# Two low-degree nodes per counting slot in a graph layer: counts in ones and 256s, copied as 16-bit integers and read as bytes

## The chip, the cores and the metric

The kernel runs on one core of a Trainium2 chip. The metric is the device time of one execution in microseconds; the median of several runs is compared. An execution that was profiled gives the profile: every instruction with its engine, start, duration and what it waited for. The engines are TensorE (PE, with weight loads shown as PEld), VectorE (DVE), ScalarE (ACT), GpSimd (POOL) and SyncE (SP). SP only issues DMAs; POOL issues the indirect ones, which gather rows.

## The reference

`x` has 12,500 nodes of 128 features. There are 200,000 edges, each with a source, a destination and one of four types; they are sorted by destination, and the destinations are dense at small numbers (the node number goes as a uniform number squared).

```
h    = max(layernorm(x), 0)
msgs = h[src] @ W[type] + b[type]          # per edge
out  = x + segment_sum(msgs, dst)
```

## The kernel before

**Two ways for edges.** The edges lie in 1563 chunks of 128. The first 464 chunks (59,392 edges, destinations below 1144) go the *dense* way, because each of these nodes has many edges: for each node the kernel counts how many edges come from each source node with each type, and multiplies the counts with the table of all `h`. The other 1099 chunks go the *gathered* way.

**The gathered way** (`gather`, line 397, and `sum_up`, line 414). POOL gathers 128 rows per chunk with one indirect DMA (line 403) into `hm`, eight chunks to a buffer, five buffers. PE sums the rows of a chunk by type and destination (line 461, one-hots made by DVE at line 424), ACT copies the sums (line 468), PE applies `W` (line 475), and DVE adds the result to a ring of destinations (line 487). Groups have 16 chunks; there are 71 groups, the last four of 12, 8, 4 and 3 chunks. The first eight groups are "raw": they gather rows of `x` and normalize them, while the table `htab` of `h`, split into three bf16 parts, is being written to DRAM. From group 8 on the rows come from `htab`.

**The dense way** (`count`, line 725, `multiply`, line 757). A *slot* is up to 128 edges of one node, one per partition. `loT` and `hkT` hold for each slot (a column) the source's row number (0 to 127) and a number made of its block (0 to 97) and the edge's type. For each slot DVE makes two one-hot tiles, 128 wide from `loT` (line 737) and 392 wide from `hkT` (line 738), and PE multiplies them (line 742): a 128 x 392 table of counts in PSUM. A few nodes have more than one slot; two slots at most accumulate into one table, and a node with more is treated as several *virtual* nodes whose results are added. ACT then copies the table as 8-bit floats into `counts` (line 745) and sums it along the way, to check that no count is too large. There are 1336 slots and 1180 virtual nodes, so 1336 pairs of one-hots and matmuls and 1180 copies.

`multiply` reads the whole table `htab` once per batch of nodes, in 25 loads of up to 384 KB on SP (line 763, five buffers), and multiplies the three parts with `counts` (line 766, 294 matmuls of up to 368 columns), then with `W` (line 779), and adds to `acc` (line 784). The 15 batches have 23, 46, eleven times 92, 53 and 46 virtual nodes.

**The order.** `dense_work` (line 806) interleaves `count` of one batch with `multiply` of the batch before, in equal progress. The main loop (line 846) goes through the groups; after each quarter of a group it takes steps of the dense work until their share of PE columns reaches `pace` (line 793), so that the sum of a group's own columns and its dense columns is the same for each group from 8 to `FULL - 3` (64). What is left is done at group 65. The slots are built during the raw groups by `make_slots` (line 599), whose last steps run just before group 8. When the dense work is done, `leave` (line 496) transposes `acc`, adds `x` and stores the rows, and `check_all` (line 554) combines the checks into one flag; if it is set, a slow and general version runs at the end.

Of the kernel before, what the change touches and what calls it, by code (L numbers as in the profile page):

```python
# [31 lines left out]
F32 = mybir.dt.float32  # L35
BF16 = mybir.dt.bfloat16
F16 = mybir.dt.float16
F8 = mybir.dt.float8e4
I32 = mybir.dt.int32
AF = mybir.ActivationFunctionType  # L40
ALU = mybir.AluOpType
AX = mybir.AxisListType
# [4 lines left out]
P = 128  # L47
# [8 lines left out]
VBMAX = 92  # L56
# [11 lines left out]
def kernel(  # L68
# [44 lines left out]
        return next((n for n in range(12, WIN, 4) if (n - 1) * a_node > P + 6 * P**0.5), WIN)  # L113

    NDT = -(-ND // P)
    virtual = [(k, d) for k in range(0, len(levels), 2) for d in range(levels[k])]

    virtual = virtual[ND - 2 * VBMAX : ND] + virtual[: ND - 2 * VBMAX] + virtual[ND:]
    VB = VBMAX
    sizes_of = [VB // 4, VB // 2]  # L120
    left = len(virtual) - sum(sizes_of) - VB // 2
    sizes_of += [VB] * (left // VB) + ([left % VB] if left % VB else []) + [VB // 2]
    batches = [virtual[sum(sizes_of[:i]) :][:n] for i, n in enumerate(sizes_of)]
    NB = NW * NT


# [427 lines left out]
    def check_all():  # L554

        low = const.tile([P, BM], F32, name="low")
        step = const.tile([P, BM], F32, name="step")
        nc.vector.memset(low, 0.0)
        for (ja, jb, _), i in zip(flushes, goes):
            if starts[i] + sizes[i] < TM:  # L560
                nc.vector.tensor_scalar(
                    step, rowf, starts[i] + sizes[i] - 0.5, (jb - ja) * float(P), ALU.is_gt, ALU.mult
                )
                nc.vector.tensor_add(low, low, step)
        bad = const.tile([P, 5], F32, name="bad")
# [10 lines left out]
        many = const.tile([P, 2], F32, name="many")  # L576
        nc.vector.tensor_reduce(many[:, 0:1], bad, AX.X, ALU.add)
        nc.vector.tensor_copy(many[:, 1:2], seen)
        pb = x_ps.tile([P, 2], F32, name="pt")
        nc.tensor.matmul(pb, ones, many, start=True, stop=True)  # L580
        sums_ok = const.tile([P, 2], F32, name="sums_ok")
        nc.vector.tensor_single_scalar(sums_ok[:, 0:1], pb[:, 0:1], 0.5, op=ALU.is_gt)
        nc.vector.tensor_single_scalar(sums_ok[:, 1:2], pb[:, 1:2], 3.0 * E0, op=ALU.not_equal)
        nc.vector.tensor_reduce(flag, sums_ok, AX.X, ALU.max)


# [12 lines left out]
    def make_slots(dix):  # L599
# [79 lines left out]
        def unpack(a, z):  # L679
            n = z - a  # L680
            hk = dix.tile([P, 512], I32, name="hk")
            nc.vector.tensor_single_scalar(hk[:, :n], packed[:, a:z], 7, op=ALU.arith_shift_right)
            nc.vector.tensor_copy(hkT[:, a:z], hk[:, :n])
            nc.vector.scalar_tensor_tensor(
                loT[:, a:z], hkT[:, a:z], float(-P), packed[:, a:z], op0=ALU.mult, op1=ALU.add
            )

            nc.vector.tensor_single_scalar(hk[:, :n], hk[:, :n], NT - 1, op=ALU.bitwise_and)
            ohs = []
            for t in range(NT):  # L690
                is_t = dix.tile([P, 512], BF16, name="is_t", bufs=NT)
                if t < NT - 1:
                    nc.vector.tensor_single_scalar(is_t[:, :n], hk[:, :n], t + 1.0, op=ALU.is_equal)
                else:
                    nc.vector.tensor_single_scalar(is_t[:, :n], hkT[:, a:z], 0.5, op=ALU.is_gt)
                ohs.append(is_t)
            yield True
            pn = x_ps.tile([N3, 512], F32, name="pt")
            for t in range(NT):
                nc.tensor.matmul(pn[:, :n], pick_a[:, t, :], ohs[t][:, :n], start=(t == 0), stop=(t == NT - 1))  # L700
            nc.scalar.copy(cnt12[:, a:z], pn[:, :n])

        for a, z in pieces(NS):
            yield from unpack(a, z)
            yield True
        nc.vector.memset(seen, 0.0)
        nc.vector.tensor_reduce(seen[:N3], cnt12, AX.X, ALU.add)

# [15 lines left out]

    def count(vs, counts):
        todo = []
        for i, (k, d) in enumerate(vs):
            todo.append((i, starts_of[k] + d, True, not (k + 1 < len(levels) and d < levels[k + 1])))
            if not todo[-1][3]:
                todo.append((i, starts_of[k + 1] + d, False, True))  # L730
        both = sdp.tile([P, VB], F32, name="both", bufs=2)
        for s0 in range(0, len(todo), OB):
            part = todo[s0 : s0 + OB]
            o1 = ohp.tile([P, OB, P], BF16, name="o1")
            o2 = ohp.tile([P, OB, NB], BF16, name="o2")
            for k, (i, s, first, last) in enumerate(part):
                nc.vector.tensor_scalar(o1[:, k, :], iota_b, loT[:, s : s + 1], None, ALU.is_equal)  # L737
                nc.vector.tensor_scalar(o2[:, k, :], iota_n, hkT[:, s : s + 1], None, ALU.is_equal)  # L738
            for k, (i, s, first, last) in enumerate(part):
                if first:  # L740
                    pb = x_ps.tile([P, NB], F32, name="pt")
                nc.tensor.matmul(pb, o1[:, k, :], o2[:, k, :], start=first, stop=last)  # L742
                if last:

                    nc.scalar.activation(  # L745
                        counts[:, :, i * NT : (i + 1) * NT],
                        pb.rearrange("p (b t) -> p b t", t=NT),
                        AF.Copy,
                        accum_out=both[:, i : i + 1],
                        saturate=True,  # L750
                    )
                yield (s0 + k + 1) / len(todo)
        top = sdp.tile([P, 1], F32, name="top")
        nc.vector.tensor_reduce(top, both[:, : len(vs)], AX.X, ALU.max)
        nc.vector.tensor_max(most, most, top)

    def multiply(vs, counts):
        nv = len(vs)
        pa = a_ps.tile([P, VB * NT], F32, name="pa")
        for j0 in range(0, NW, HB):  # L760
            j1 = min(j0 + HB, NW)
# [10 lines left out]
                    )  # L772
            if j1 < NW:
                yield j1 / NW
        sd = sdp.tile([P, VB, NT], F32, name="sd")
        nc.scalar.copy(sd[:, :nv].rearrange("p v t -> p (v t)"), pa[:, : nv * NT])
        py = y_ps.tile([P, VB], F32, name="py")
        for t in range(NT):
            nc.tensor.matmul(py[:, :nv], wsb[:, t, :], sd[:, :nv, t], start=(t == 0), stop=(t == NT - 1))  # L779
        i = 0  # L780
        while i < nv:
            k, d = vs[i]
            n = next((m for m in range(1, nv - i) if vs[i + m] != (k, d + m)), nv - i)
            nc.vector.tensor_tensor(acc[:, d : d + n], acc[:, d : d + n], py[:, i : i + n], ALU.add)
# [7 lines left out]

    def pace(gi, part):

        last = FULL - 2
        if gi >= last:
            return 2.0
        own = [columns(i) for i in range(RAW, last)]
# [2 lines left out]
        return ((n + part) * a_group - sum(own[:n]) - part * own[n]) / dense_columns()  # L801

    def dense_columns():
        return NS * float(NB) + len(virtual) * NW * 3.0 * NT

    def dense_work():

# [5 lines left out]
        for vs in batches + [None]:  # L813
            steps = {}
            now = None
            if vs:
                now = vs, dense.tile([P, NW, VB * NT], F8, name="counts")
                slots = sum(1 + (k + 1 < len(levels) and d < levels[k + 1]) for k, d in vs)
                steps[count(*now)] = slots * a_slot
# [12 lines left out]
            before = now  # L832

    seen = const.tile([P, 1], F32, name="seen")
    slots = mid.enter_context(tc.tile_pool(name="slots", bufs=1, side="right"))
    loT = slots.tile([P, NS], F32, name="loT")
    hkT = slots.tile([P, NS], F32, name="hkT")
    building = ExitStack()
    dix = building.enter_context(tc.tile_pool(name="dix", bufs=1, side="right"))
    to_slots = make_slots(dix)  # L840
# [5 lines left out]
    for gi, (t0, g) in enumerate(zip(starts, sizes)):  # L846
# [85 lines left out]
        if gi == RAW - 1:  # L932
# [11 lines left out]
            most = sdp.tile([P, 1], F32, name="most")  # L944
            nc.vector.memset(most, 0.0)
            work = dense_work()
        for (ja, jb, _), i in zip(flushes, goes):
            if i == gi:
# [135 lines left out]
```

## Time and profile before

| | |
|---|---|
| median of 3 runs | 1467.21 us (1465.16 to 1470.11) |
| profiled execution, its own time | 1466.72 us |
| its span, first to last instruction | 1465.0 us |
| mean granted PE clock | 0.950 |
| busy: PE, DVE, ACT, POOL | 1305.8, 1055.8, 860.7, 1078.9 us |
| HBM read and written | 263.84 MB, 16.03 MB |

The page of the profile lists, for groups of instructions, the line, engine and operation, the tiles written and read, shapes, how often, then busy time, mean duration in ns, and idle time of the engine before them with what ended it. Durations of neighbouring instructions on one engine can overlap, so that starts, not durations, tell how often an engine takes one. The row of tenths gives busy shares in 40 slices of the run.

### The profile page before, as it was taken

What the parts mean: (1) busy time and instruction counts of PE and PEld (TensorE: products, weight loads), DVE (VectorE), ACT (ScalarE), POOL (GpSimd) and SP (SyncE); (2) the same over time, 40 slices, a digit from 0 to 9 for tenths busy, and PEclk for the clock granted to TensorE, in tenths of its full rate; (3) what the DMA queues carried; (4) which work ended last, traced back from release to release, by engine and by line L of the source; (5) the groups of instructions that cost most, each with busy time, mean ns of one, the idle gap of its engine ahead of it and who ended that gap; (6) DMA issues with size and microseconds to landing.
All of it is one profiled execution on the core that took longest, in us unless ns stands there. A gap on an engine that the chain in (4) does not pass through costs nothing.

```text
span 1465.0 us, 32946 instructions
## 1 busy us (share of the span) xinstructions
PE 1305.8 (89%) x10222; PEld 866.6 (59%) x10222; DVE 1055.8 (72%) x5728; ACT 860.7 (59%) x3026; POOL 1078.9 (74%) x1109
## 2 busy tenths in 40 slices
PE   1566787998999999999999999999999999999964
PEld 0444455765666556666666666666666666677743
DVE  8796878879889877677675786757787676677233
ACT  7776447867545566566655666646766665445010
POOL 7777775677677767777777777777777777777773
PEclk9995768999999999999999999999999999999977
DMA  7643247975566567676676767776676667777841
GB/s 214 181 138 115 89 149 245 299 231 173 154 193 176 165 183 204 190 225 200 202 205 196 210 186 207 199 200 201 192 209 193 190 194 212 216 237 252 304 121 54
DMA packets 141833, 282.11 MB, mean 193 GB/s; under 512 B 26995, under 2 KB 74661, under 8 KB 141653
## 3 DMA queue, kind: packets, MB, share of 16 engines
q1 hardware_dynamic: 90949, 176.07, 38.3%
q0 software_dynamic: 50704, 103.91, 26.3%
q8 instruction: 80, 1.31, 0.3%
q14 instruction: 100, 0.82, 0.2%
HBM read 263.84 MB, written 16.03 MB: 191 GB/s over the span
## 4 chain that ended last, share of the span: by engine, by line
PE 70%; DVE 11%; ACT 4%; DMA 3%; POOL 2%; issue 2%; DVEq 0%; ACTq 0%; POOLq 0%
PE pa L766 35%; PE pt L742 13%; PE py L475 9%; PE ps L461 8%; ACT counts L745 3%; DVE o L738 3%; DVE o L737 2%; POOL hm L403 2%; DVE ring L487 2%; DMA hs<-htab 2%; DVE oh L424 2%; DMA hm<-htab,srcT 1%; PE ps L444 1%; PE ps L446 1%; PE py L779 1%
## 5 line engine op out<-in xcount | busy, mean ns | idle before, releaser
L403 POOL DMA_INDIRECT hm<-htab,srcT x971 | 947.0, 975 | 322.4 <-issue 266.9
L766 PE MATMUL pa<-counts,hs 128*128 128x368 fp8e4 (+3 forms) x4410 | 713.2, 299 | 7.2 <-DMA hs<-htab 6.4
L745 ACT ACTIVATE counts<-pt 128x392 fp8e4<-128x392 f32 x1180 | 574.7, 519 | 169.7 <-PE pt L742 165.8
L766 PEld LDWEIGHTS <-hs 128*128 128x128 bf16 x4410 | 404.3, 99 | 232.4 <-issue 31.7
L738 DVE TENSOR_SCALAR o<-iota_n,hkT 128x392 bf16<-128x392 f16 x1336 | 450.3, 337 | 0.0
L737 DVE TENSOR_SCALAR o<-iota_b,loT 128x128 bf16<-128x128 bf16 x1336 | 346.8, 260 | 128.5 <-PE pt L742 126.7
L742 PE MATMUL pt<-o,o 128*128 128x392 bf16 x1336 | 368.0, 333 | 11.4 <-ACT counts L745 3.9
L745 ACT ACTIVATION_READ_ACCUMULATOR counts<-pt 128x1 f32 x1180 | 268.7, 228 | 0.0
L487 DVE TENSOR_TENSOR ring<-ring,py 128x16 f32 (+4 forms) x1072 | 187.3, 175 | 106.8 <-PE py L475 89.8
L468 ACT COPY sb<-ps 128x320 f32<-128x320 f32 (+4 forms) x275 | 115.8, 424 | 234.1 <-PE ps L461 210.0
L424 DVE TENSOR_SCALAR oh<-iota_b,keyT 128x64 bf16<-128x64 bf16 (+4 forms) x971 | 179.2, 265 | 90.1 <-PE ps L461 88.2
L461 PE MATMUL ps<-oh,hm 128*128 128x80 bf16 (+4 forms) x2913 | 160.0, 202 | 20.9 <-DMA hm<-htab,srcT 19.8
L461 PEld LDWEIGHTS <-hm 128*128 128x128 bf16 x2913 | 136.8, 99 | 59.1 <-DMA hm<-htab,srcT 26.2
L742 PEld LDWEIGHTS <-o 128*128 128x128 bf16 x1336 | 125.5, 99 | 78.0 <-DVE o L738 13.0
L475 PE MATMUL py<-sb,wsb 128*128 128x384 f32 (+4 forms) x536 | 170.9, 454 | 0.3 <-ACT sb L468 0.3
L403 POOL DMA_INDIRECT hm<-in_x_dram,srcT x128 | 130.4, 1019 | 40.8 <-issue 36.9
L475 PEld LDWEIGHTS py<-sb,wsb 128*128 128x128 f32 x536 | 107.0, 211 | 38.3 <-issue 13.7
L450 ACT CAST cnt<-ps 128x256 bf16<-128x256 f32 (+7 forms) x71 | 29.3, 413 | 130.0 <-PE ps L446 112.4
L461 PE MATMUL ps<-ohf,hm 128*128 128x48 f32 x256 | 59.0, 391 | 51.5 <-ACT hm L365 51.5
L461 PEld LDWEIGHTS ps<-ohf,hm 128*128 128x128 f32 x256 | 52.8, 298 | 69.0 <-ACT hm L365 55.7
L365 ACT ACTIVATE hm<-hm,nmr,rstd 128x128 f32<-128x128 f32 x128 | 51.0, 481 | 6.3 <-DVE nmr L356 6.3
L473 PE MATMUL py<-cnt,b 128*128 128x256 bf16 (+5 forms) x67 | 20.7, 309 | 24.0 <-DVE ring L487 22.8
(173 smaller groups left out, 551.7 us busy)
## 6 DMA issues: line engine op xcount, KB each, us to landing
hs<-htab SPq DMA_DIRECT2D x360, 384.0 KB
hm<-htab,srcT POOLq DMA_INDIRECT x971
htab<-h SPq DMA_DIRECT2D x11, 768.0 KB
xo<-in_x_dram SPq DMA_DIRECT2D x23, 256.0 KB
out_dram<-xo SPq DMA_DIRECT2D x23, 256.0 KB
xt<-in_x_dram SPq DMA_DIRECT2D x6, 512.0 KB
hs<-htab SPq DMA_DIRECT2D x15, 192.0 KB
xt<-in_x_dram SPq DMA_DIRECT2D x5, 448.0 KB
```

Of the source, the lines that this page charges most:

```text
L365: nc.scalar.activation(h(k), xt(k), AF.Relu, bias=nmr[:r, k : k + 1], scale=rstd[:r, k : k + 1])
L403: nc.gpsimd.indirect_dma_start(out=rows[:, (i - h0) * width : (i - h0 + 1) * width], out_offset=None, in_=table, in_offset=bass.IndirectOf ...
L424: nc.vector.tensor_scalar(oh[:, i, :], (iota_f if raw else iota_b)[:, :K], keyf[:, t0 + i : t0 + i + 1], None, ALU.is_equal)
L461: mm = nc.tensor.matmul(ps[:, i - i0, :], rows(i, c, nparts), oh[:, i, :], start=(c == 0), stop=(c == nparts - 1),)
L468: nc.scalar.copy(sb[:, i0:i1].rearrange("p g t n -> p g (t n)"), ps[:, : i1 - i0, :])
L475: mm = nc.tensor.matmul(py[:, :g, :], wsb[:, t, :], sb[:, :g, t, :], start=False, stop=(t == NT - 1))
L487: nc.vector.tensor_tensor(to, to, py[:, i, :], ALU.add)
L737: nc.vector.tensor_scalar(o1[:, k, :], iota_b, loT[:, s : s + 1], None, ALU.is_equal)
L738: nc.vector.tensor_scalar(o2[:, k, :], iota_n, hkT[:, s : s + 1], None, ALU.is_equal)
L742: nc.tensor.matmul(pb, o1[:, k, :], o2[:, k, :], start=first, stop=last)
L745: nc.scalar.activation(counts[:, :, i * NT : (i + 1) * NT], pb.rearrange("p (b t) -> p b t", t=NT), AF.Copy, accum_out=both[:, i : i + 1], ...
L766: nc.tensor.matmul(pa[:, : nv * NT], hs[:, j - j0, c * D : (c + 1) * D], counts[:, j, : nv * NT], start=(j == 0 and c == 0), stop=(j == NW ...
```

## The change

**Pairs.** Nodes from `PAIRS` = 558 up to 1143 have so few edges that two neighbours together fit 128 partitions. As edges are sorted, the edges of the two lie in different partitions of their two columns, so the columns of `loT` and `hkT` are added into one, and `byT` holds 1 in the partitions of the first node and 256 in those of the second. One pair of one-hots and one matmul then count both; the one-hot from `loT` is multiplied by `byT`. The other ("alone") nodes are also put in twos: each keeps its own slots, the second's one-hots are multiplied by the constant 256, and both accumulate into the same table.

**One copy for two.** The table holds (ones) + 256 x (the second's). ACT copies it once as 16-bit unsigned integers. `multiply` reads the same bytes as 8-bit floats: the low byte is the first node, the high byte the second. A byte n up to 16, read as such a float, is n / 512, so the later copy scales by 512. The sums along the way are taken apart with integer operations on DVE at the end of a batch, and a further check compares the total number of counted edges with the expected one.

**Order.** The first two batches (22 and 46 nodes) take shared pairs only; the others mix alone and shared nodes in proportion. There are 1043 slots and 590 copies. Slots per batch: before 23, 46, 92, 161, 160, eight times 92, 53, 65; after 11, 23, 121, 121, 107, then 70 or 71 eight times, 52, 44. `pace` spreads the dense work over one group more (`FULL - 1`). The one-hots of `make_slots` share a pool of buffers.

```diff
+    PAIRS = next(
+        d
+        for d in range(levels[1] + levels[1] % 2, ND, 2)
+        if (lambda m: m + 6 * m**0.5)(E * (((d + 2) / N) ** 0.5 - (d / N) ** 0.5)) <= P
+    )
+    alone = [(k, d) for k in range(0, len(levels), 2) for d in range(min(levels[k], PAIRS))]
+    shared = [(0, d) for d in range(PAIRS, ND)]
...
+    sizes_of = [VB // 8 * 2, VB // 4 * 2]
+    left = len(alone) + len(shared) - sum(sizes_of) - VB // 4 * 2
+    sizes_of += [VB] * (left // VB) + ([left % VB] if left % VB else []) + [VB // 4 * 2]
+    batches = []
+    a = b0 = 0
+    for i, n in enumerate(sizes_of):
+        na, ns = len(alone) - a, len(shared) - b0
+        n1 = 0 if i < 2 else min(round(n * na / (na + ns) / 2) * 2, na)
+        n1 = max(n1, n - ns)
+        batches.append(alone[a : a + n1] + shared[b0 : b0 + n - n1])
+        a, b0 = a + n1, b0 + n - n1
...
+    def slots_of(u):
+        if u[0] is not None and u[0][0] == 0 and u[0][1] >= PAIRS:
+            return [(u[0][1], None)]
+        got = []
+        for v, by in zip(u, (1.0, 256.0)):
+            if v is not None:
+                k, d = v
+                got.append((starts_of[k] + d, by))
+                if k + 1 < len(levels) and d < levels[k + 1]:
+                    got.append((starts_of[k + 1] + d, by))
+        return got
...
+        one, two = slice(PAIRS, ND, 2), slice(PAIRS + 1, ND, 2)
+        nc.vector.tensor_scalar(byT, hkT[:, two], 0.5, 255.0, ALU.is_gt, ALU.mult)
+        nc.vector.tensor_single_scalar(byT, byT, 1.0, op=ALU.add)
+        for of in (loT, hkT):
+            nc.vector.tensor_tensor(of[:, one], of[:, one], of[:, two], ALU.add)
...
-                nc.vector.tensor_scalar(o1[:, k, :], iota_b, loT[:, s : s + 1], None, ALU.is_equal)
+                if by == 1.0:
+                    nc.vector.tensor_scalar(o1[:, k, :], iota_b, loT[:, s : s + 1], None, ALU.is_equal)
+                else:
+                    if by is None:
+                        by = byT[:, (s - PAIRS) // 2 : (s - PAIRS) // 2 + 1]
+                    nc.vector.tensor_scalar(o1[:, k, :], iota_b, loT[:, s : s + 1], by, ALU.is_equal, ALU.mult)
                 nc.vector.tensor_scalar(o2[:, k, :], iota_n, hkT[:, s : s + 1], None, ALU.is_equal)
...
                         accum_out=both[:, i : i + 1],
-                        saturate=True,
...
-        nc.vector.tensor_reduce(top, both[:, : len(vs)], AX.X, ALU.max)
-        nc.vector.tensor_max(most, most, top)
+        n = len(vs) // 2
+        nc.vector.tensor_copy(bi[:, :n], both[:, :n])
+        nc.vector.tensor_single_scalar(bb[:, 0, :n], bi[:, :n], 255, op=ALU.bitwise_and)
+        nc.vector.tensor_single_scalar(bb[:, 1, :n], bi[:, :n], 8, op=ALU.arith_shift_right)
+        nc.vector.tensor_copy(bf[:, :, :n], bb[:, :, :n])
+        nc.vector.tensor_reduce(top[:, 0:1], bf[:, :, :n], AX.XY, ALU.max)
+        nc.vector.tensor_reduce(top[:, 1:2], bf[:, :, :n], AX.XY, ALU.add)
+        nc.vector.tensor_max(most, most, top[:, 0:1])
+        nc.vector.tensor_add(held, held, top[:, 1:2])
...
+        counts = counts.bitcast(F8)
...
-        nc.scalar.copy(sd[:, :nv].rearrange("p v t -> p (v t)"), pa[:, : nv * NT])
+        nc.scalar.activation(
+            sd[:, : nv // 2].rearrange("p v t m -> p (v t m)"), pa[:, : nv * NT], AF.Copy, scale=512.0
+        )
...
-        last = FULL - 2
+        last = FULL - 1
...
-                now = vs, dense.tile([P, NW, VB * NT], F8, name="counts")
+                now = vs, dense.tile([P, NW, VB // 2 * NT], U16, name="counts")
```

More of the change, by code (lines that the diff above doesn't have):

```diff
@@ L39 @@
 I32 = mybir.dt.int32
+U16 = mybir.dt.uint16
 AF = mybir.ActivationFunctionType
@@ L115, with units @@
     NDT = -(-ND // P)
-    virtual = [(k, d) for k in range(0, len(levels), 2) for d in range(levels[k])]
-    virtual = virtual[ND - 2 * VBMAX : ND] + virtual[: ND - 2 * VBMAX] + virtual[ND:]
-    VB = VBMAX
[L120 to L123, printed above, removed]
+    PAIRS = next(
[4 more added lines that the diff above has]
+    alone = [(k, d) for k in range(0, len(levels), 2) for d in range(min(levels[k], PAIRS))]
+    if len(alone) % 2:
+        alone.append(None)
+    shared = [(0, d) for d in range(PAIRS, ND)]
+    VB = VBMAX
+    sizes_of = [VB // 8 * 2, VB // 4 * 2]
[9 more added lines that the diff above has]
+        a, b0 = a + n1, b0 + n - n1
+    assert a == len(alone) and b0 == len(shared)
+    def slots_of(u):
[9 more added lines that the diff above has]
+        return got
+    def units(vs):
+        return [tuple(vs[i : i + 2]) for i in range(0, len(vs), 2)]
+    NSLOTS = sum(len(slots_of(u)) for vs in batches for u in units(vs))
     NB = NW * NT
@@ L575, in check_all @@
         nc.vector.tensor_single_scalar(bad[:, 4:5], most, MANY + 0.5, op=ALU.is_gt)
-        many = const.tile([P, 2], F32, name="many")
+        many = const.tile([P, 3], F32, name="many")
         nc.vector.tensor_reduce(many[:, 0:1], bad, AX.X, ALU.add)
         nc.vector.tensor_copy(many[:, 1:2], seen)
-        pb = x_ps.tile([P, 2], F32, name="pt")
+        nc.vector.tensor_copy(many[:, 2:3], held)
+        pb = x_ps.tile([P, 3], F32, name="pt")
         nc.tensor.matmul(pb, ones, many, start=True, stop=True)
-        sums_ok = const.tile([P, 2], F32, name="sums_ok")
+        sums_ok = const.tile([P, 3], F32, name="sums_ok")
         nc.vector.tensor_single_scalar(sums_ok[:, 0:1], pb[:, 0:1], 0.5, op=ALU.is_gt)
         nc.vector.tensor_single_scalar(sums_ok[:, 1:2], pb[:, 1:2], 3.0 * E0, op=ALU.not_equal)
+        nc.vector.tensor_single_scalar(sums_ok[:, 2:3], pb[:, 2:3], float(E0), op=ALU.not_equal)
         nc.vector.tensor_reduce(flag, sums_ok, AX.X, ALU.max)
@@ L690, in unpack @@
             for t in range(NT):
-                is_t = dix.tile([P, 512], BF16, name="is_t", bufs=NT)
+                is_t = dix.tile([P, 512], BF16, name="sel", bufs=2 * DENSE)
                 if t < NT - 1:
@@ L726, in count @@
         todo = []
[L727 to L731, printed above, removed]
+        for i, u in enumerate(units(vs)):
+            of = slots_of(u)
+            todo += [(i, c, by, n == 0, n == len(of) - 1) for n, (c, by) in enumerate(of)]
+        both = sdp.tile([P, VB // 2], F32, name="both", bufs=2)
         for s0 in range(0, len(todo), OB):
@@ L735, in count @@
             o2 = ohp.tile([P, OB, NB], BF16, name="o2")
-            for k, (i, s, first, last) in enumerate(part):
-                nc.vector.tensor_scalar(o1[:, k, :], iota_b, loT[:, s : s + 1], None, ALU.is_equal)
+            for k, (i, s, by, first, last) in enumerate(part):
+                if by == 1.0:
[4 more added lines that the diff above has]
+                    nc.vector.tensor_scalar(o1[:, k, :], iota_b, loT[:, s : s + 1], by, ALU.is_equal, ALU.mult)
                 nc.vector.tensor_scalar(o2[:, k, :], iota_n, hkT[:, s : s + 1], None, ALU.is_equal)
-            for k, (i, s, first, last) in enumerate(part):
+            for k, (i, s, by, first, last) in enumerate(part):
                 if first:
@@ L749, in count @@
                         accum_out=both[:, i : i + 1],
-                        saturate=True,
                     )
                 yield (s0 + k + 1) / len(todo)
-        top = sdp.tile([P, 1], F32, name="top")
-        nc.vector.tensor_reduce(top, both[:, : len(vs)], AX.X, ALU.max)
-        nc.vector.tensor_max(most, most, top)
+        n = len(vs) // 2
+        bi = sdp.tile([P, VB // 2], I32, name="bi")
+        nc.vector.tensor_copy(bi[:, :n], both[:, :n])
+        bb = sdp.tile([P, 2, VB // 2], I32, name="bb")
+        nc.vector.tensor_single_scalar(bb[:, 0, :n], bi[:, :n], 255, op=ALU.bitwise_and)
+        nc.vector.tensor_single_scalar(bb[:, 1, :n], bi[:, :n], 8, op=ALU.arith_shift_right)
+        bf = sdp.tile([P, 2, VB // 2], F32, name="bf")
+        nc.vector.tensor_copy(bf[:, :, :n], bb[:, :, :n])
+        top = sdp.tile([P, 2], F32, name="top")
+        nc.vector.tensor_reduce(top[:, 0:1], bf[:, :, :n], AX.XY, ALU.max)
+        nc.vector.tensor_reduce(top[:, 1:2], bf[:, :, :n], AX.XY, ALU.add)
+        nc.vector.tensor_max(most, most, top[:, 0:1])
+        nc.vector.tensor_add(held, held, top[:, 1:2])
     def multiply(vs, counts):
         nv = len(vs)
+        counts = counts.bitcast(F8)
         pa = a_ps.tile([P, VB * NT], F32, name="pa")
@@ L774, in multiply @@
                 yield j1 / NW
-        sd = sdp.tile([P, VB, NT], F32, name="sd")
-        nc.scalar.copy(sd[:, :nv].rearrange("p v t -> p (v t)"), pa[:, : nv * NT])
+        sd = sdp.tile([P, VB // 2, NT, 2], F32, name="sd")
+        nc.scalar.activation(
+            sd[:, : nv // 2].rearrange("p v t m -> p (v t m)"), pa[:, : nv * NT], AF.Copy, scale=512.0
+        )
         py = y_ps.tile([P, VB], F32, name="py")
         for t in range(NT):
-            nc.tensor.matmul(py[:, :nv], wsb[:, t, :], sd[:, :nv, t], start=(t == 0), stop=(t == NT - 1))
+            nc.tensor.matmul(py[:, :nv].rearrange("p (v m) -> p v m", m=2), wsb[:, t, :], sd[:, : nv // 2, t, :], start=(t == 0), stop=(t == NT - 1))
         i = 0
         while i < nv:
+            if vs[i] is None:
+                i += 1
+                continue
             k, d = vs[i]
@@ L803, in dense_columns @@
     def dense_columns():
-        return NS * float(NB) + len(virtual) * NW * 3.0 * NT
+        return NSLOTS * float(NB) + sum(len(vs) for vs in batches) * NW * 3.0 * NT
     def dense_work():
@@ L816, in dense_work @@
             if vs:
-                now = vs, dense.tile([P, NW, VB * NT], F8, name="counts")
-                slots = sum(1 + (k + 1 < len(levels) and d < levels[k + 1]) for k, d in vs)
-                steps[count(*now)] = slots * a_slot
+                now = vs, dense.tile([P, NW, VB // 2 * NT], U16, name="counts")
+                steps[count(*now)] = sum(len(slots_of(u)) for u in units(vs)) * a_slot
             if before:
@@ L834 @@
     seen = const.tile([P, 1], F32, name="seen")
+    most = const.tile([P, 1], F32, name="most")
+    held = const.tile([P, 1], F32, name="held")
+    for t in (most, held):
+        nc.vector.memset(t, 0.0)
     slots = mid.enter_context(tc.tile_pool(name="slots", bufs=1, side="right"))
@@ L837 @@
     hkT = slots.tile([P, NS], F32, name="hkT")
+    byT = slots.tile([P, (ND - PAIRS) // 2], F32, name="byT")
     building = ExitStack()
@@ L943 @@
             hsp = mid.enter_context(tc.tile_pool(name="hsp", bufs=5))
-            most = sdp.tile([P, 1], F32, name="most")
-            nc.vector.memset(most, 0.0)
             work = dense_work()
```

## The prediction

> **What bounds the kernel now.** I read the page first, then the waits of GpSimd (POOL), then POOL in order of time, then a table of stretches. On the page TensorE (PE) looks like the bound: 1305.8 of 1465.0 us busy. But its "mean ns of one" overlap, and the POOL row says something else.
>
> ```profile
> PE   1566787998999999999999999999999999999964
> ...
> POOL 7777775677677767777777777777777777777773
> ...
> L403 POOL DMA_INDIRECT hm<-htab,srcT x971 | 947.0, 975 | 322.4 <-issue 266.9
> ...
> L745 ACT ACTIVATE counts<-pt 128x392 fp8e4<-128x392 f32 x1180 | 574.7, 519 | 169.7 <-PE pt L742 165.8
> ...
> L738 DVE TENSOR_SCALAR o<-iota_n,hkT 128x392 bf16<-128x392 f16 x1336 | 450.3, 337 | 0.0
> L737 DVE TENSOR_SCALAR o<-iota_b,loT 128x128 bf16<-128x128 bf16 x1336 | 346.8, 260 | 128.5 <-PE pt L742 126.7
> L742 PE MATMUL pt<-o,o 128*128 128x392 bf16 x1336 | 368.0, 333 | 11.4 <-ACT counts L745 3.9
> ...
> L403 POOL DMA_INDIRECT hm<-in_x_dram,srcT x128 | 130.4, 1019 | 40.8 <-issue 36.9
> ```
>
> POOL issues 1099 gathers (971 + 128), one per chunk of edges. Each is followed by 0.30 us put down to "issue", that is, to no wait. A typical one lasts 0.946 us (the median; the mean is 0.975), so an unhindered gather comes every 1.25 us. The first starts at 4.1 us, the last at 1441.9: 1437.8 us for 1098 intervals. 1098 x 1.25 = 1373. The other 65 us are gathers that lasted longer than 0.946 (1077.4 busy - 1099 x 0.946 = 38 us) and real waits, about 27 us. So **POOL is never idle for more than 27 us in the whole run**, and 22 us after its last gather the kernel is done. In order of time:
>
> ```profile
> 245.26 1.01 POOL L403 DMA_INDIRECT hm<-htab,srcT  x1 [0.30 <-issue]
> 258.68 1.06 POOL L403 DMA_INDIRECT hm<-htab,srcT  x1 [12.42 <-PE ps L461]
> 260.05 0.95 POOL L403 DMA_INDIRECT hm<-htab,srcT  x1 [0.30 <-issue]
> ...
> 281.10 0.98 POOL L403 DMA_INDIRECT hm<-htab,srcT  x1 [1.88 <-PE pa L766]
> ...
> 373.71 0.94 POOL L403 DMA_INDIRECT hm<-htab,srcT  x1 [6.57 <-PE pt L742]
> ...
> 543.77 0.94 POOL L403 DMA_INDIRECT hm<-htab,srcT  x1 [3.77 <-PE pt L742]
> ```
>
> In brackets stands the idle time before a gather and what ended it. These, with 1.78, 1.06, 0.84 and 0.70 us elsewhere, are all waits above 0.6 us: 29.0 - 8 x 0.3 = 26.6 us. POOL waits there for PE to release one of the five row buffers (40 chunks). After 544 us it never waits again: PE follows the gathers, 34 chunks behind at 658 us and 17 behind at 1330 us. **PE can only shorten the run through those 27 us.**
>
> ```profile
> 200.00:250.00 50.00, 42.34 (x367) 28.55 (x367) 38.90 (x208) 35.46 (x132) 34.81 (x36) 0.76 0.64 213
> 250.00:300.00 50.00, 45.38 (x535) 36.37 (x535) 41.26 (x220) 40.75 (x164) 30.59 (x31) 0.97 0.90 291
> 350.00:400.00 50.00, 45.11 (x356) 28.04 (x355) 45.32 (x247) 28.42 (x100) 33.69 (x34) 0.97 0.54 152
> ...
> 1400.00:1450.00 50.00, 29.36 (x173) 17.30 (x171) 14.77 (x78) 6.21 (x14) 32.45 (x35) 0.69 0.40 107
> ```
>
> Columns: PE, PE weight load, DVE, ACT, POOL busy, then granted clock, DMA share, GB/s. The early waits have three causes: DMA at 0.90 (250 to 300), ACT at 41 of 50, and from 350 DVE at 45 of 50.
>
> **Removed.** The loop bounds give 1336 slots before and 1043 after, 1180 copies before and 590 after.
> - PE: 293 matmuls. Back to back beside L766 they take 0.166 us (starts at 907.15, 907.32, 907.48), so 293 x 0.166 = 49 us.
> - ACT: copy with accumulator read repeats every 0.47 us (starts at 217.24, 217.72, 218.19), so 590 x 0.47 = 277 us.
> - DVE: a pair L737 and L738 repeats every 0.43 us (from 211.29 to 213.85, six pairs), so 293 x 0.43 = 126 us.
>
> None of this shortens the end by itself. What counts is when a row buffer comes free before 544 us.
>
> **The first wait (12.1 us net).** Group 8 runs from 216.4 to 252.4 us, and POOL needs the buffer that the first half of group 9 frees. The pace of before gives group 8 43638 - 6912 = 36726 dense columns: 9016 for the first batch's 23 slots, the rest 61% of second count plus first multiply (45080), so 15.4 of its 25 loads of 384 KB. The trace agrees: 15 loads are used before group 9. After, it gets 41153 - 6912 = 34241 columns, 4312 go to 11 slots, and 29929 of 34888 is 86%: 21.4 loads. With five loaded ahead, the loads come every 1.35 us there (uses at 238.85 to 248.27, DMA saturated). Six more cost 8.1 us; 12 fewer copies let the multiply begin 5.6 us earlier; 3.1 us in which PE waited for DVE's L424 before group 9 probably go. Sum -0.6, between -6 and +4: I take this wait as **unchanged**.
>
> **The other waits (14.5 us net).** 1.3 us of them belong to the table's writes and to the raw part and stay. The others fall in batches 3 to 5: before 92, 161 and 160 slots with 92 copies each, after 121, 121 and 107 with 46 each. DVE need per group at 350 us: before 36726 / 171304 x 161 = 34.5 slots x 0.43 = 14.8 us plus 16 x (0.155 + 0.09) = 3.9 for L424 and L487, plus flushes: close to POOL's 20.4 us per group. After, 34241 / 155624 x 121 = 26.6 slots: 11.4 + 3.9. The cover is there. Batch 3 is tight: 34241 / 101528 x 121 = 41 slots x 0.43 + 3.9 = 21.5 us per group for three groups, some 3 us too slow, but 12 us of stall just taken give it slack. I take 1.5 us as left: **-12 us**.
>
> **Slower gathers.** The 38 us above 0.946 lie where DVE is busy; in the last 50 us, with DVE at 14.77, gathers take 0.94 to 0.95. DVE loses 126 of about 1056 us: 38 x 0.12 = **-4 us** (0 to -8).
>
> **Added.** (a) Half of the remaining L737 (668) also multiply, most by a column. No row has that form. The nearest two-operation row, L240 (128 elements, an int32 operand), has 341 ns against 260, so 0 to +0.08 us each, 53 us in all. [...] At +0.08, batch 3's 20 such slots per group cost 1.6 us a group, 5 us of wait: kept in the range. (b) Six more small DVE operations per batch at about 0.2 us (L754 244 ns, L755 154): 18 us, hidden by DVE's idle time; without that cover, 18 us. (c) Four operations that build byT and add columns at some 200 us, about 2 us ahead of the first count, in the -6 to +4 above. (d) 16-bit output: same 392 elements, ACT time follows elements: 0, bounds -0.05 to +0.1 us; ACT has 277 us to spare. (e) A third check column: under 1 us.
>
> **Moved.** The dense work ends one group later (FULL - 1), and with it on SP three loads and stores of acc (L501, L514), behind which the last ring flushes queue, nine transposes and four DVE adds. Before, it ended at 1391 us, with 59 chunks to come; now 43, at about 1395. PE took 7.3 us for the 16 chunks of group 65 (1391.6 to 1399.0), so 43 cost it 20 us, and POOL is busy until about 1427. I take **+1 us** (-1 to +5).
>
> **Sum.** Against the profiled execution (span 1465.0, itself 1466.7): -12 - 4 + 1 = -15, so a span of 1450. The median of the runs, 1467.2, is 2.2 above the span: **1452 us**.
>
> **Rivals.**
> 1. *All waits go*: the first multiply starts as soon as eleven copies are done and group 9 comes early. -26 - 7 - 1 gives about 1433. For it: ACT is nearly full from 217 to 225. Against it: DMA is at 1.0 in that stretch and needs the same bytes. Chance 0.12.
> 2. *Nothing changes*: the extra loads in group 8 lengthen the first wait by what the others give back, or two-operation L737 keeps DVE late: 1463 to 1471. Chance 0.13.
> 3. *Slower, by the clock*. From 550 to 1350 us PE is busy 792 of 800. After, it needs about 0.74 us less per group (21 slots of 92 fewer per batch, 4.7 groups per batch), 19.0 us against POOL's 20.4, and idles in front of late gathers. If the granted clock drops below 19.0 / 20.4 = 0.93, PE sets the pace. The row is 42.34 busy with 0.76, 45.38 with 0.97. [...] At a held 0.90 it would be 21.1 x 57 groups, +40 us, less the 15: about 1490. [...] Chance 0.06.
> 4. *The counters don't add up* and the slow path runs: many times 1467. Chance 0.01, in no range.
>
> **How the numbers follow.** My forecast has 0.68, own range 1443 to 1462. A measurement of this kernel tells about 0.3%, 4.4 us: under 1462.8 is faster. Faster: 0.68 + 0.12 = 0.80; same 0.12, slower 0.08 (rivals 3 and 4, and a bad tail). The range leaves out half of rival 1 and the slow cases: 1437 to 1466.
>
> **What would show it.** Right: x1043 on L737, L738 and L742, x590 on the copy; POOL's wait near 258 us still some 10 to 13 us, and no wait above 2 us at 370 and 540; from then on gathers every 1.25 us; PE with waits for hm throughout; the last gather near 1427 us and the end 22 to 24 us behind it. Wrong, if the last gather comes at 1440 or later (waits elsewhere), if the tail behind it grows by over 5 us, if L737 averages over 340 ns, or if the clock is under 0.93 between 550 and 1350.

## The result, and the profile after

The changed kernel takes **1450.14 us** (median of 4 runs, 1447.92 to 1452.02), against 1466.18 us (1462.83 to 1470.11) for the kernel before beside it. The ratio is 0.9889, with a 95% interval of 0.9859 to 0.9919. The forecast was 1452 us, and the time is inside its range.

The page of the profiled execution (1448.84 us, span 1447.1, mean granted clock 0.929) has these rows. The first is POOL's busy share in 40 slices; the others are groups of instructions in the form of the page shown before.

```profile
POOL 7777777567777777777777777777777777777773
PE 54%; POOL 17%; issue 8%; DVE 7%; DMA 5%; ACT 2%; DVEq 0%; POOLq 0%; ACTq 0%
...
L440 POOL DMA_INDIRECT hm<-htab,srcT x971 | 939.2, 967 | 313.3 <-issue 276.1
L794 ACT ACTIVATE counts<-pt 128x392 uint16<-128x392 f32 x590 | 290.3, 505 | 277.9 <-PE pt L791 276.3
L787 DVE TENSOR_SCALAR o<-iota_n,hkT 128x392 bf16<-128x392 f16 x1043 | 342.4, 328 | 0.2 <-issue 0.2
L791 PE MATMUL pt<-o,o 128*128 128x392 bf16 x1043 | 270.0, 336 | 4.3 <-ACT counts L794 2.0
...
L782 DVE TENSOR_SCALAR o<-iota_b,loT 128x128 bf16<-128x128 bf16 x375 | 97.8, 261 | 95.7 <-PE pt L791 94.3
L440 POOL DMA_INDIRECT hm<-in_x_dram,srcT x128 | 130.3, 1018 | 40.8 <-issue 36.6
...
L786 DVE TENSOR_SCALAR o<-iota_b,loT,byT 128x128 bf16<-128x128 bf16 x293 | 98.7, 337 | 28.5 <-PE pt L791 28.1
...
L786 DVE TENSOR_SCALAR o<-iota_b,loT 128x128 bf16<-128x128 bf16 x375 | 98.0, 261 | 4.0 <-PE pt L791 3.9
```

The counts are as planned: 1043 slots, 590 copies. The copies still cost about the same each (505 ns, before 519): in the kernel before, ACT's copies of sums take 378 ns for 256 elements and 486 for 384, and 375 and 492 with bf16 output, so its time grew with the elements there and hardly changed with the output. ACT lost 283 us of work (860.7 busy before, 577.5 after), DVE 100 us and PE 53 us. The run lost 16. The 1099 gathers are still there, and nearly nine tenths of the idle time in front of those from `htab` is still the fixed 0.30 us of "issue". The second row is the chain that ended last, as shares of the span. Before, it read:

```profile
PE 70%; DVE 11%; ACT 4%; DMA 3%; POOL 2%; issue 2%; DVEq 0%; ACTq 0%; POOLq 0%
```

POOL's share rose from 2% to 17%. PE still has the largest share, because it nearly always has work waiting (busy for 1252.5 of 1447.1 us); what would shorten the run can't be read from the chain, and the experiments below ask it.

As in the prediction, POOL's run from its first gather to its last can be taken apart: 1098 intervals of 1.25 us, waits beyond the usual 0.3 us, and the time by which gathers lasted longer than 0.946 us. The "tail" is what lies behind the start of the last gather.

| us | last gather starts | waits | longer gathers | tail | span |
|---|---|---|---|---|---|
| before | 1441.9 | 27.0 | 37.8 | 23.1 | 1465.0 |
| after | 1424.7 | 17.8 | 29.8 | 22.4 | 1447.1 |
| difference | -17.2 | -9.2 | -8.0 | -0.7 | -17.9 |

POOL in order of time, with the idle time before a gather and its releaser in brackets, shows where the waits are now:

```profile
278.98 0.95 POOL L440 DMA_INDIRECT hm<-htab,srcT  x1 [10.98 <-PE ps L498]
...
302.34 0.94 POOL L440 DMA_INDIRECT hm<-htab,srcT  x1 [3.04 <-PE ps L498]
...
325.37 0.94 POOL L440 DMA_INDIRECT hm<-htab,srcT  x1 [2.50 <-PE ps L498]
...
336.86 0.94 POOL L440 DMA_INDIRECT hm<-htab,srcT  x1 [0.88 <-PE pt L791]
```

The waits of 6.57 and 3.77 us near 374 and 544 are gone; these four and one of 0.61 us at 347 are all waits above 0.6 us behind 250 us. A long first wait is still there, at 279 instead of 259. The one near 303 grew from 1.78 to 3.04, and one near 325 is new.

Stretches of the changed kernel (columns: PE, PE weight load, DVE, ACT, POOL busy, granted clock, DMA share, GB/s):

```profile
250.00:300.00 50.00, 44.18 (x436) 34.76 (x435) 43.61 (x233) 15.40 (x54) 29.74 (x30) 0.91 0.79 258
350.00:400.00 50.00, 50.00 (x426) 33.09 (x425) 43.19 (x249) 14.50 (x49) 38.31 (x39) 1.00 0.66 196
800.00:850.00 50.00, 29.92 (x248) 18.74 (x246) 16.64 (x105) 13.40 (x44) 37.82 (x41) 0.72 0.45 131
```

ACT fell from 41 of 50 to 15 in the first stretch. From 350 us POOL gathers without a pause (39 gathers, 38.31 busy; before 34 and 33.69). In the third PE has caught up with the gathers and is busy for 30 of 50 us. POOL does not notice: 41 gathers.

### The profile page after: what moved, and what is told of

It reads as the page before. It is cut to its first block, busy times and chain, and to the rows that moved or that the text cites. A ratio compares the mean times of both kernels' runs of the same rounds, so it can differ in the third digit from the quotient of the medians.

```text
span 1447.1 us, 30717 instructions
## 1 busy us (share of the span) xinstructions
PE 1252.5 (87%) x9929; PEld 844.2 (58%) x9929; DVE 956.1 (66%) x5251; ACT 577.5 (40%) x1846; POOL 1071.0 (74%) x1109
## 4 chain that ended last, share of the span: by engine, by line
PE 54%; POOL 17%; issue 8%; DVE 7%; DMA 5%; ACT 2%; DVEq 0%; POOLq 0%; ACTq 0%
PE pa L826 27%; POOL hm L440 17%; PE pt L791 8%; PE py L512 7%; PE ps L498 7%; DMA hm<-htab,srcT 3%; ACT counts L794 2%; DMA hs<-htab 1%; DVE ring L524 1%; DVE o L787 1%; PE ps L481 1%; PE pt L546 1%; DVE o L786 1%; PE py L841 1%; DVE oh L461 1%
## 5 line engine op out<-in xcount | busy, mean ns | idle before, releaser
L826 PE MATMUL pa<-counts,hs 128*128 128x368 fp8e4 (+3 forms) x4410 | 680.6, 301 | 10.8 <-DMA hs<-htab 9.1
L794 ACT ACTIVATE counts<-pt 128x392 uint16<-128x392 f32 x590 | 290.3, 505 | 277.9 <-PE pt L791 276.3
L787 DVE TENSOR_SCALAR o<-iota_n,hkT 128x392 bf16<-128x392 f16 x1043 | 342.4, 328 | 0.2 <-issue 0.2
L791 PE MATMUL pt<-o,o 128*128 128x392 bf16 x1043 | 270.0, 336 | 4.3 <-ACT counts L794 2.0
L498 PE MATMUL ps<-oh,hm 128*128 128x80 bf16 (+4 forms) x2913 | 169.7, 204 | 68.0 <-DMA hm<-htab,srcT 66.9
L498 PEld LDWEIGHTS <-hm 128*128 128x128 bf16 x2913 | 137.4, 100 | 114.6 <-DMA hm<-htab,srcT 82.4
L782 DVE TENSOR_SCALAR o<-iota_b,loT 128x128 bf16<-128x128 bf16 x375 | 97.8, 261 | 95.7 <-PE pt L791 94.3
L440 POOL DMA_INDIRECT hm<-in_x_dram,srcT x128 | 130.3, 1018 | 40.8 <-issue 36.6
L791 PEld LDWEIGHTS <-o 128*128 128x128 bf16 x1043 | 96.1, 100 | 50.0 <-issue 5.2
L794 ACT ACTIVATION_READ_ACCUMULATOR counts<-pt 128x1 f32 x590 | 124.2, 211 | 0.0
L786 DVE TENSOR_SCALAR o<-iota_b,loT,byT 128x128 bf16<-128x128 bf16 x293 | 98.7, 337 | 28.5 <-PE pt L791 28.1
L498 PE MATMUL ps<-ohf,hm 128*128 128x48 f32 x256 | 59.9, 393 | 51.0 <-ACT hm L402 50.9
L786 DVE TENSOR_SCALAR o<-iota_b,loT 128x128 bf16<-128x128 bf16 x375 | 98.0, 261 | 4.0 <-PE pt L791 3.9
L498 PEld LDWEIGHTS ps<-ohf,hm 128*128 128x128 f32 x256 | 53.3, 300 | 69.7 <-ACT hm L402 55.4
```

Source lines behind the costliest of these rows:

```text
L440: nc.gpsimd.indirect_dma_start(out=rows[:, (i - h0) * width : (i - h0 + 1) * width], out_offset=None, in_=table, in_offset=bass.IndirectOf ...
L498: mm = nc.tensor.matmul(ps[:, i - i0, :], rows(i, c, nparts), oh[:, i, :], start=(c == 0), stop=(c == nparts - 1),)
L794: nc.scalar.activation(counts[:, :, i * NT : (i + 1) * NT], pb.rearrange("p (b t) -> p b t", t=NT), AF.Copy, accum_out=both[:, i : i + 1],)
L826: nc.tensor.matmul(pa[:, : nv * NT], hs[:, j - j0, c * D : (c + 1) * D], counts[:, j, : nv * NT], start=(j == 0 and c == 0), stop=(j == NW ...
```

## The experiments

**Four runs on a chip that was slower.** Four variants of the changed kernel ran on it: 310 more matmuls (pe_back), a second copy of each table (act_back), 30 gathers fewer (skip30), fewer table loads in the first two multiplies (half_loads). On that chip the kernel before took 2218.24 us instead of 1467, so the times can't be read against the forecasts. Waits between engines lasted longer in all four: where ACT had waited for the sums of four chunks, its copy started 3.0 to 3.7 us (median) behind the last matmul that it needs, against 0.04 us in the changed kernel elsewhere. Why is open. The forecast for the one that ran only there:

> The changed kernel, with each of the 590 copies done twice: 277 us of ScalarE work, as much as the change took away, given back. The result is the same numbers. Gather theory: only the first groups can feel it (34 copies more before the second multiply, 16 us of ScalarE beside a DMA-bound stretch): +0 to +6 us, the wait of POOL near 279 us at most 5 us longer, the gathers behind 400 us unhindered. Rival, that halving the copies is what gained: the whole gain is lost, 1464 to 1468.

```diff
+                    nc.scalar.activation(
+                        counts[:, :, i * NT : (i + 1) * NT],
+                        pb.rearrange("p (b t) -> p b t", t=NT),
+                        AF.Copy,
+                        accum_out=both[:, i : i + 1],
+                    )
```

The four took 2082.48, 2126.1, 2022.75 and 2055.87 us. POOL in order of time, in pe_back, shows why these times say little of the others:

```profile
706.79 0.95 POOL L440 DMA_INDIRECT hm<-htab,srcT  x1 [6.78 <-PE ps L498]
708.05 0.95 POOL L440 DMA_INDIRECT hm<-htab,srcT  x1 [0.31 <-issue]
...
718.92 0.95 POOL L440 DMA_INDIRECT hm<-htab,srcT  x1 [2.31 <-PE ps L498]
```

A gather costs the same 0.95 + 0.30 us as elsewhere, but POOL waits for PE in front of the buffers all along; its waits sum to 616 to 685 us in a run. act_back came 44 us behind pe_back there, and what those 44 us were was not followed. It is the only run with the copies doubled; on a chip at the usual speed it was not tried. The other three ran again on chips where the kernel before took 1466.97 to 1467.42 us.

**310 matmuls more.** This tells POOL from PE as the bound, since it gives PE back what the change took.

> The same edit as pe_back (293 count matmuls of 0.166 us more, 49 us of TensorE work, in the batches from the sixth on; same numbers come out), on a chip that runs the kernel before at about 1467 us. Gather theory: hidden in TensorE's 67 us of waits for gathers, 1447 to 1456 us, last gather near 1425 us. Rival, TensorE's work made the gain: 1485 to 1500 us.

```diff
+        late = batches.index(vs) >= 5
...
+                if first and late and i % 10 < 7:
+                    nc.tensor.matmul(pb, o1[:, k, :], o2[:, k, :], start=True, stop=True)
```

Measured 1450.85 us (1450.07 to 1455.33), ratio to before 0.9901 (0.9876 to 0.9926): 0.7 us over the changed kernel, within its spread. PE's waits say where the matmuls went (waited for: us in all, times, longest). Changed kernel:

```profile
PE ps L498 <- DMA hm<-htab,srcT: 66.9, 79, 2.9
```

With 310 matmuls more:

```profile
PE ps L498 <- DMA hm<-htab,srcT: 38.8, 42, 2.8
```

In the kernel before:

```profile
PE ps L461 <- DMA hm<-htab,srcT: 19.8, 22, 2.1
```

PE's saving lies in front of late gathers as idle time; given back, it goes back to work there (PE is busy 32 us more, and these waits are 28 us shorter). In the late batches PE, the busiest engine of the page, isn't the bound.

**30 gathers fewer.** The last chunk of 30 of the groups from htab is not gathered; the second-last chunk's rows are used in its place.

> The same edit as skip30 (30 of 1099 gathers left out, groups 30 to 59; their matmuls read the rows of the chunk before), on a chip that runs the kernel before at about 1467 us. Gather theory: 28 to 37 us less than the changed kernel's 1450, so 1413 to 1422 us. If another engine sets the end: 1445 to 1451 us.

```diff
+        skip = table is htab and 30 * G <= t0 < 60 * G
...
-            for i in range(h0, min(h0 + HG, g)):
+            for i in range(h0, min(h0 + HG, g) - (skip and h0 > 0)):
```

```profile
L441 POOL DMA_INDIRECT hm<-htab,srcT x941 | 912.4, 970 | 304.3 <-issue 264.3 <-PE ps L500 18.1 <-PE pt L793 7.4
```

Measured 1413.57 us (1413.02 to 1414.97), 36.6 us under the changed kernel: 1.22 us for each gather, against 1.25 by the rows. POOL's waits (18.0) and longer gathers (31.5) stay as they were. The number of gathers sets the run.

**Half the table loads of the first two multiplies.** Loads with even numbers stay; 24 of 50 are left out, and the matmuls use the tile loaded last. Counts are multiplied with wrong rows there.

> The same edit as half_loads (24 of 50 table loads left out in the first two multiplies; the matmuls use the load before), on a chip that runs the kernel before at about 1467 us. If the loads filling the DMA engines make the long wait of POOL (11.0 us near 279 us): under 3 us there and 1439 to 1444 us. If VectorE or ScalarE makes it: 1448 to 1450 us. The waits near 302 and 325 us, put down to VectorE, stay within 2 us.

```diff
+            if j0 // HB % 2 == 0 or batches.index(vs) > 1:
                 hs = hsp.tile([P, HB, D3], BF16, name="hs")
                 nc.sync.dma_start(hs[:, : j1 - j0, :], ...)
```

Measured 1440.66 us (1436.96 to 1442.65), ratio 0.9825 (0.9795 to 0.9854). POOL in order of time:

```profile
291.03 0.94 POOL L440 DMA_INDIRECT hm<-htab,srcT  x1 [0.60 <-PE ps L498]
...
314.19 0.94 POOL L440 DMA_INDIRECT hm<-htab,srcT  x1 [2.62 <-PE ps L498]
...
325.66 0.94 POOL L440 DMA_INDIRECT hm<-htab,srcT  x1 [0.88 <-PE pt L791]
```

Gather by gather, the wait of 10.98 us is gone (the same gather starts at 268.4 here, behind the usual 0.30), and the next one, 3.04 us near 302, is down to 0.60. That was not expected to move by more than 2 us. The two behind it, 2.50 and 0.88, stay (2.62 and 0.88). So the table loads make the first wait and most of the second. In the changed kernel the DMA share is 0.95 from 225 to 275 us; here it is 0.74.

**Less dense work in the groups with waits.** The change, with 12,000 columns taken from each of the groups 8 to 13 and spread over the rest:

> The changed kernel with 12000 columns less of dense work in each of the groups 8 to 13 and some 1240 more in each group (a gentler start of the dense work; nothing left out). On a chip that runs the kernel before at about 1466 us: if the waits of POOL between 250 and 350 us (17.8 us beyond the ordinary gaps in the changed kernel) come from dense work crowded into these groups, they fall to some 3 us and the run takes 1433 to 1439 us, while TensorE, at 19.5 us a group, still stays under POOL's 20.2. If TensorE's work sets the end, nothing or a loss: 1447 to 1470 us. If waits between engines last as long as in the four runs before (kernel before at 2218 us): 0.92 to 0.95 of the time before, for want of those waits' shares, and the theories are not told apart.

```diff
-        own = [columns(i) for i in range(RAW, last)]
+        own = [columns(i) + (12000 if i < RAW + 6 else 0) for i in range(RAW, last)]
```

Measured **1437.69 us** (1434.97 to 1440.59), before 1467.9, ratio 0.9794 (0.9768 to 0.9821): faster than both kernels. POOL's waits for PE:

```profile
POOL hm L440 <- PE pt L791: 6.1, 20, 0.3
...
POOL hm L440 <- PE ps L498: 3.7, 12, 0.3
```

None is over the 0.3 us that every gather has. Waits beyond that fell from 17.8 to 1.1 us, longer gathers stay at 32.1, and the last gather starts at 1410.5, 14.2 us earlier: most of what POOL lost to waits has come back.

**The same pacing without the change.**

> The kernel before with only the gentler start of the dense work (12000 columns less in each of the groups 8 to 13). If early crowding is all: the 16 us of waits up to 310 us go, 1448 to 1452 us, as good as the change. If the slots matter too, as the prediction has it (VectorE at 45 of 50 us from 350 us on, TensorE 19.8 us per group against POOL's 20.4, now 20.3): the waits near 370 and 540 us stay or grow and TensorE can't make up for them, 1454 to 1462 us.

The edit is that one line, in the kernel before. Measured 1449.11 us (1447.81 to 1451.14), before 1466.97, ratio 0.988 (0.9859 to 0.9901). I had expected the late waits to stay, and they did not. All waits above 0.6 us behind 240 us are:

```profile
252.05 0.94 POOL L403 DMA_INDIRECT hm<-htab,srcT  x1 [5.04 <-PE ps L461]
...
893.12 0.95 POOL L403 DMA_INDIRECT hm<-htab,srcT  x1 [3.42 <-PE pt L742]
```

Waits fell from 27.0 to 9.4 us, more than by the whole change, while longer gathers stay at 39.4. The waits near 374 and 544 us are gone, but one of 3.42 us came at 893, where the kernel before had none. The late waits of before are no property of batches 3 to 5 alone: near 544 us this kernel has more dense work than before, and no wait. But PE did not catch up: at 1330 us it was 30 chunks behind, before 17. One constant gives what the change gives. With both, the medians show another 11.4 us; the profiled spans differ by 15.5 us, 8.3 of it in waits (9.4 to 1.1) and 7.3 in gathers (39.4 to 32.1).

**Half the copies alone.** Twos of nodes share a table, but no slots are merged: 1336 slots, 590 copies.

> One part of the change alone: two nodes per copy, in ones and 256s, but no shared slots. 1336 pairs of one-hots and count matmuls as before, 590 copies as after; the single-slot nodes of the first batches are chosen as before. Gather theory: halving copies doesn't help where VectorE is late, so the waits of POOL near 370 and 540 us come back (10 us) and the gathers are stretched as before (some 37 us in all): 1460 to 1468 us. Rival, that the halved copies (277 us of ScalarE) made the gain: 1448 to 1454 us.

```diff
-    PAIRS = next(
-        d
-        for d in range(levels[1] + levels[1] % 2, ND, 2)
-        if (lambda m: m + 6 * m**0.5)(E * (((d + 2) / N) ** 0.5 - (d / N) ** 0.5)) <= P
-    )
+    PAIRS = ND
...
+    alone = alone[ND - 2 * VBMAX : ND] + alone[: ND - 2 * VBMAX] + alone[ND:]
```

Measured 1462.09 us (1455.21 to 1469.83, 7 runs), before 1466.97, ratio 0.996 (0.9931 to 0.9989). The time is the expected one, the way to it is not. POOL in order of time near the places of the late waits, and then its gathers:

```profile
366.77 0.95 POOL L437 DMA_INDIRECT hm<-htab,srcT  x1 [1.66 <-PE ps L495]
...
473.47 0.94 POOL L437 DMA_INDIRECT hm<-htab,srcT  x1 [1.95 <-PE pt L783]
```

```profile
L437 POOL DMA_INDIRECT hm<-htab,srcT x971 | 952.9, 981 | 311.8 <-issue 271.0 <-PE ps L495 16.4 <-PE pt L783 11.1
```

Waits fell by 10.6 us to 16.4, as much as with the whole change, but gathers got longer by 5.8 us (43.6, before 37.8). The wait near 374 is down from 6.57 to 1.66, the one near 544 is gone, and one of 1.95 near 473 is new. So in this profile the shorter waits come with the fewer copies, and the shorter gathers only with the fewer slots: 13.8 us between this kernel and the changed one. (It also has the change's `pace` and batch sizes, 1.4% less dense work in group 8 than before. It is one profile of a kernel whose runs lie 14.6 us apart.) DVE, which I had named, is as busy from 350 to 400 us as before (45.33 of 50, 45.32 before), and most of the wait is gone all the same.

**DVE's operations and the gathers.** Which DVE operations make gathers longer? 660 operations that the rest doesn't need were added to late batches, in two kinds.

> The changed kernel with one more VectorE operation per slot in the batches from the sixth on (660 in all): a 128-wide bf16 tensor_scalar of the form of the one-hots, SBUF to SBUF, into a tile that nobody reads; some 0.16 us each, 106 us of VectorE, which idles 40% there. Same numbers come out. In the changed kernel a gather behind 350 us lasts 0.945 us with no tensor_scalar beside it, 0.954 with four and 1.02 with eight. If such operations hold up POOL (theory: 8 of the 18 us gained are gathers that VectorE no longer stretches): gathers together 4 to 10 us longer (excess over 0.946 from 30 to 34 to 40 us), and the run 4 to 10 us longer. If the stretching only comes at the same time as VectorE's work, from DMA traffic: 0 to 1 us.

> As dve_fast, but the 660 operations are tensor_reduce (maximum) over the same 128 bf16 numbers to one, some 0.2 us each: more VectorE time in a form with one result. Same numbers come out. If it is the form of the fast tensor_scalar that holds up POOL: 0 to 1.5 us longer. If any VectorE work does: at least as much as dve_fast, 5 to 13 us.

```diff
+                if late:
+                    nc.vector.tensor_scalar(o3, iota_b, 1.0, None, ALU.mult)
```

and, in the other kernel, `tensor_reduce(o3[:, 0:1], iota_b, AX.X, ALU.max)`. Measured 1450.4 us (1449.41 to 1450.96) and 1448.94 us (1448.0 to 1449.82). The first:

```profile
L440 POOL DMA_INDIRECT hm<-htab,srcT x971 | 939.1, 967 | 314.2 <-issue 275.8 <-PE ps L498 20.0 <-DMA hm<-htab,srcT 5.8
...
L791 DVE TENSOR_SCALAR o<-iota_b 128x128 bf16<-128x128 bf16 x660 | 138.5, 210 | 2.0 <-DVE ring L524 0.2
```

Longer gathers sum to 29.7 and 28.1 us, without the operations 29.8. Neither kind lengthens the gathers, though DVE is busy 66 and 111 us more. The added `tensor_scalar` isn't quite the form of the one-hots: it reads no column, and the next operation starts 0.10 us behind it (median), not 0.16. So a 128-wide operation of 0.10 us by itself doesn't hold up POOL; that the one-hots do, which read a column and feed matmuls, is not excluded.

## Why the prediction was right, point by point

**The bound: right.** POOL's gathers set the end: 30 left out save 36.6 us. That PE's 49 us do not shorten it by themselves is shown by the 310 matmuls given back, which cost 0.7 us, and for DVE by the reductions, 111 us of busy time that cost nothing; both were added to the late batches alone. ACT's 277 us were not given back on a chip of the usual speed. Taking them away alone gained 4.9 us.

**The first wait, "unchanged": right in size by luck, wrong in place.** It was 12.1 us beyond the 0.3 and is 10.7. The sum had 21.4 loads used in group 8 and POOL waiting for group 9. The trace has 21 loads in use by 250.7 us. But the 48 matmuls that sum group 9 stand in PE's order among the matmuls of loads 13 to 16 (240.9 to 243.4 us), not behind those of all 21, so their buffers came free early. The delay stands before group 10 instead, which begins at 275.0 (before 277.0), and the wait is at 279 instead of 259. The sum was made for a wait that did not come, so that its size fits the other one is luck. That the loads cause the one that came is shown by leaving half of them out.

**The other waits, -12: direction right, too large.** The ones near 374 and 544 us went. But 5.8 us of waits beyond 0.3 were left (near 302, 325, 337 and 347, in batch 3, called tight, and just behind it) instead of 1.5; DVE is busy 43.61 of 50 us from 250 and 42.73 from 300. The first of the four shrank by 2.4 us with half the loads, so DVE is not its main cause. These other waits changed by -7.8, and all waits with the first by -9.2.

The reason given, DVE's need of 14.8 + 3.9 of 20.4 us per group, is the step that failed: with the copies alone halved DVE stayed as busy and the wait near 374 fell to 1.66 us, and with the pacing alone, with all DVE operations as before, both late waits were gone. What makes them is not shown. A backlog fits: POOL waits where PE is more than 32 chunks behind as a new buffer is due, and with the pacing alone PE is less far behind (28 chunks at 365 us and 26 at 500, before 39 and 33). For the one near 544 this does not come from less work there, since the pacing puts more dense work there. For the one near 374 the pacing also took work away close by, so the two aren't told apart. PE did not catch up afterwards either, and the wait at 893 us came.

**Slower gathers, -4 (0 to -8): at the end of its range.** It was -8.0. Kernels with 1336 slots have 37.8, 39.4 and 43.6 us of it, those with 1043 slots 28 to 32. So it goes with slots, more than with DVE's busy time, which fell by only a tenth. That is a match of two sizes, not a cause; what in a slot does it stays open. The extra 128-wide operations, which read no column, do not. The 392-wide one-hot, the matmul with its table, or what these do to memory were not told apart; nor was it settled why halving the copies alone raised it.

**The two-operation one-hot, 0 in the sum: half right.** No run shows that 0 for the form with a column, and no row of before has either form: it was my estimate. With the constant 256 the form repeats every 0.162 us, like the plain one (375 instances each). With a column as second operand it takes 0.223 (293 instances). So the second operation costs nothing with a constant, and +0.06 us with a column, inside the 0 to +0.08 that was kept. The 668 two-operation forms are 64% of the slots, not half, and 293 of them, not most, have a column. These 293 are 18 us of DVE, and their share of the waits near 302 and 325 was not measured by itself.

**The tail, +1: measured -0.7.** The dense work ended at 1401.2 us, not 1395, with the same 43 chunks ahead of PE, 24 of them already gathered. By 1415 us PE was 3 chunks behind the gathers. POOL was busy until 1425.7, so the six us cost nothing.

**The sum.** -15 forecast, -17.9 in the profiled executions and -16.0 in the medians. The terms were further off than the sum: the first wait 0 forecast and -1.4 measured, the other waits -12 and -7.8, the gathers -4 and -8.0, the tail +1 and -0.7. The two large errors cancel. How much of the gain the change's own `pace` over one group more and its new order of the batches make was not measured by itself.

**Rivals.** *All waits go* did not come: DMA kept a long first wait, as the argument against it said (its share was 1.00 from 238 to 249 us before, and is 0.95 from 225 to 275 after); with the other pacing the waits do go. *Nothing changes* is excluded by the interval. *The counters don't add up* did not come. *The clock* came in its first half: PE idles in front of late gathers, in 79 waits of up to 2.9 us, and the granted clock does fall. From 822.5 to 853 us it is 0.50:

```profile
822.50:853.00 30.50, 13.36 (x92) 8.40 (x92) 7.91 (x47) 5.65 (x18) 23.15 (x25) 0.50 0.32 88
```

Half the clock begins at 822.46 us, near the end of a wait of 2.85 us (the next matmul starts at 822.65), and goes on through waits of 0.3 to 1.3 us in a thinly busy PE. From 819.06 to 822.46 us PE was busy for 0.50 us. The rival's two rows, 0.76 and 0.97 in stretches with PE busy for 42.34 and 45.38 of 50 us, did not tell of this: the stretch around it, 800 to 850 us, has 29.92 busy and 0.72, though from 550 to 1350 us the mean is 0.95. It cost nothing: POOL made 25 gathers in these 30.5 us, and PE was waiting for gathers all that time and stayed 2 to 5 chunks behind. It fell behind only afterwards, to 26 chunks at 880 us, with the clock back at 1.00:

```profile
853.00:880.00 27.00, 27.00 (x170) 16.87 (x170) 16.84 (x95) 8.63 (x31) 20.34 (x22) 1.00 0.72 220
```

In that time PE did dense work and summed hardly a chunk (5 matmuls of L498 from 853.9 to 879.9 us). This comes from the order of its work: in the kernel before, at clock 1.00, PE sums none from 864.5 to 895 us. A second such stretch, half clock from 1290 to 1314 us, is followed by the same, up to 28 of the 40 chunks that the five buffers hold. POOL has to wait when it needs a new buffer and PE is more than 32 behind. What half a clock for that long would cost amid dense work, no run here shows.

## What to carry to other kernels

An engine that shows 74% busy can be the bound: take the count of its instructions times its undisturbed interval, and what is left over are the only waits that work elsewhere can win back. Look for where those waits begin before you make work cheaper; here one constant in the pacing was worth as much as removing a fifth of the slot matmuls and half the copies. The buffers decide how far an engine off the path may fall behind before the bound one waits, so follow the distance over time, and see what it is doing when the distance grows.

## What the hardware showed that I had not expected

- An indirect gather of 128 rows costs POOL 0.946 to 0.949 us (median) and then 0.30 us that no wait explains, in every kernel and on every chip here, the one that ran the kernel before in 2218 us included. On that chip it was the waits between engines that grew: where ACT waited for PE's sums, its copy started 3.0 to 3.7 us (median) behind the last matmul, against 0.04 elsewhere.
- PE at half clock for 30 us with no wait over 2.9 us: 0.50 us busy from 819.06 to 822.46 us, then 13.36 of 30.5 us.
- A second operand that is a column adds 0.06 us to a 128-wide bf16 one-hot; a constant adds nothing (0.162 us with it and without). The added operation without any column repeats every 0.10 us, with one column it is 0.16, with two 0.22.
- 660 further DVE operations of 0.10 us each (starts apart), or as many reductions of 280 ns, leave the length of the gathers as it was.
